# Self-attention of a decoder layer: the far corner of the weights moved to key quarters by transfers, outputs over 128 keys there, and a new written order

## The chip, the core and the metric

The kernel runs on one core of one Trainium2 chip. The metric is the device time of one execution in microseconds, lower is better. A core has five engines with queues of their own: TensorE (PE; its weight loads are shown as PEld), VectorE (DVE), ScalarE (ACT), GpSimd (POOL) and SyncE (SP), which here only issues transfers (DMAs). Everything is in float32.

## The reference

One decoder layer with normalization after each part: causal self-attention with rotary positions, cross-attention to a short context, and a feed-forward layer that only half of the tokens take. Two sequences of 1024 tokens, 256 channels, 16 heads of 64. The change touches the self-attention alone:

```python
q = split_heads(x @ Wq)
k = split_heads(x @ Wk)
v = split_heads(x @ Wv)
q = apply_rope(q)
k = apply_rope(k)
sim = jnp.einsum('bid,bjd->bij', q, k) * scale
causal = jnp.tril(jnp.ones((t, t), dtype=bool))
sim = jnp.where(causal[None], sim, -jnp.inf)
attn = jax.nn.softmax(sim, axis=-1)
out = jnp.einsum('bij,bjd->bid', attn, v)
out = out.reshape(b, h, t, d).transpose(0, 2, 1, 3).reshape(b, t, h * d)
return out @ Wo + bo
```

## The kernel before

Self-attention works on 16 pairs of heads (8 for each sequence), numbered n = 0 to 15; class `Pair` has a method for each step, and a step is written with a letter and digits. The 1024 tokens are eight tiles of 128. The steps of one pair:

- `Pk0`, `Pk1`, `Pq0`, `Pq1` (`project`, L268): keys and queries, half of the tokens each. `E..` (L276) takes them from PSUM on ScalarE; `d0`, `d1` (`swap`) send them through two transfers each so that neighbouring rows change places (`turned`); `c`, `s`, `a` (L288, L291, L295) apply the rotary tables on GpSimd.
- `Pv0`, `Pv4` (`values`, L303) and `Ev0`, `Ev4` (`kept`): values, a token tile of 128 keys on 128 partitions. `w` (`spread`) writes them to DRAM, and `l` (`copies`, L322) loads them back as `v4`, once for each of the four groups of 32 partitions: in row group r lie 32 keys of each quarter of a tile.
- `S0` to `S4` (`scores`, L342): scores of five groups of query tiles, (3, 1, 0), (4, 2), (5), (6), (7), both heads, 64 partitions each, into two PSUM tiles of which there are only two. `Tgj` (`least`, L355, VectorE) masks group g of head j, takes the row minima and frees the PSUM tile; `Xgj` (`exponentials`, L363, ScalarE) makes weights of them; `Rgj` (`turn`, L372, VectorE) writes them transposed in blocks of 32 x 32 into `p_t`. A block transpose leaves the query's quarter in the partition group and the key's quarter in the free index, so that of 128 keys only 32 stand on one group of partitions.
- `V0` to `V7` (`output`, L410): step n multiplies the weights of key tile n with its values. For key quarter k, head j and row group r there is one matmul of 32 keys by 64 columns, 32 in a step (20 in V7), and eight of them can run at once (four row groups, two column halves). Row group r adds into its own PSUM tile `po[r]`; the four take the whole ring of PSUM buffers from V0 to `O0` to `O3` (`gathered`, L424).
- `Q`, `I`, `D`, `B`, `M`, `W`: sums of the weights transposed, inverted, written to DRAM, loaded over the head's rows (`over`), multiplied in on GpSimd, and the pair's output stored.

Each of these matmuls is two instructions for TensorE, with a weight load each. The order of the work on all engines is written by hand. The list `steps` is one period, with the offset of the pair that each step works on: while the scores of pair n are made, V0 to V7 work on pair n-1 and the projections on pairs n+1 and n+2. The strings `opening` and `ending` spell out the first pairs and the last two, together with the output projection of the second sequence (`Closing`; letters A, C, Y, Z for the first sequence, f, F, g, z for the second, and U, which moves a projection from PSUM). The output projection of the first sequence, and its normalization, runs within the periods from pair 8 on. `2=` in the ending is two unread matmuls (`fill`).

`split` cuts some matmuls of scores and projections into two or four pieces, at most `pieces[n]` extra ones in pair n. `begin` issues a transfer on SyncE and, after V1 and V7, makes the next one wait for the outputs' last instruction (`gate`). SyncE, ScalarE's queue of transfers and the tables stand in program order: a waiting transfer holds up those behind it on its engine.

In the pools before, `p_t` is `[P, (NT + 1) * NT, P]`: 72 blocks, head 0 in an upper triangle (key tile, query tile), head 1 in the lower one. The constants `causal`, `ones`, `earlier` and the tiles `b2`, `w_r` live through the whole kernel; `ones`, `earlier`, `b2` and `w_r` are used only by the router and the feed-forward layer, after cross-attention has begun.

Of the kernel before, what the change touches and what calls it, by code (L numbers as in the profile page):

```python
# [34 lines left out]
def decoder_layer(  # L35
# [42 lines left out]

    ident = const.tile([P, P], F32)
    make_identity(nc, ident)  # L80
    causal = const.tile([P, P], F32)
    make_causal_mask(nc, causal, MASKED)
    neg_half = const.tile([P, 1], F32)
    G.memset(neg_half, -0.5)
    ones = const.tile([P, P], F32)
    G.memset(ones, 1.0)
    earlier = const.tile([P, P], F32)
    make_upper_triangular(nc, earlier, diag=False)
    place = const.tile([P, NT], F32)
    G.iota(place, [[P, NT]], 0, 1, allow_small_or_imprecise_dtypes=True)  # L90

# [36 lines left out]
        return po  # L128

    bo = const.tile([P, C], F32)  # L130
    b2 = const.tile([P, C], F32)
    b_r = const.tile([P, 1], F32)
    b1 = const.tile([P, NF], F32)
    w_r = const.tile([P, C], F32)
    cx = const.tile([S, B, C], F32)


# [1 line left out]

    keys = [(b, hp) for b in range(B) for hp in range(NP)]  # L140
    groups = [(3, 1, 0), (4, 2), (5,), (6,), (7,)]
    K4 = T // R32
    early = ctx.enter_context(ExitStack())
    e1 = early.enter_context(tc.tile_pool(name="early1", bufs=1, side="right"))
    e2 = early.enter_context(tc.tile_pool(name="early2", bufs=2, side="right"))
    with (
# [8 lines left out]

        fence = s1.tile([P, T], F32, name="fence")
        G.memset(fence[:, : T - P], 0.0)
        G.tensor_copy(fence[:, T - P :], causal)
        wo = s1.tile([P, NP, C], F32, name="wo")

        p_t = s1.tile([P, (NT + 1) * NT, P], F32, name="pT")
        attn_d = [dram.tile([NP, P, T], F32, tag="attn", name="attn_d") for _ in range(B)]
        x_ts = {}
        xs = [xpool.tile([P, NT, C + 1], F32, tag="x", name="x_0")]
# [1 line left out]
        def load(t, src):  # L166
            return lambda: nc.sync.dma_start(t, src)


        def load_next(h):  # L170
            if h == 0:
# [7 lines left out]
            0: [lambda: load_next(0)],  # L179
            1: [lambda: load_next(1)],  # L180
            2: [load(bo, L0_attn_bo.partition_broadcast(P))],
            3: [load(b2, L0_ffn_b2.partition_broadcast(P)), load(b_r, L0_ffn_b_r.partition_broadcast(P))],
            4: [
                load(w_r, L0_ffn_w_r.rearrange("c o -> (o c)").partition_broadcast(P)),
                load(b1, L0_ffn_b1.rearrange("(f p) -> p f", p=P)), load(cx, ctx_1024.rearrange("b s c -> s b c")),
            ],
            5: [load(wo[:, : NP // 2, :], outward[:, : NP // 2, :])],
# [29 lines left out]
        def begin(dst, src):  # L217

            ins = nc.sync.dma_start(dst, src)
            if gate:  # L220
                tc.add_manual_dep(ins.ins, gate.pop().ins.name, after, reason="the outputs' instructions come first")
# [3 lines left out]

        pieces = [2, 1, 13, 13, 11, 10, 11, 12, 13, 12, 8, 9, 8, 8, 9, 0]
        left = [pieces[0]]

        def split(first, last, most):
# [14 lines left out]
        class Pair:  # L246
# [60 lines left out]

            def kept(self, n):
                if self.v is None:
                    self.v = e1.tile([P, NT, P], F32, tag="v", name="v")  # L310
                    self.v_d = dram.tile([4, R32, NT * P], F32, tag="v", name="v_d")
                A.copy(self.v[:, n : n + NT // 2, :], self.pp["v", n])

            def spread(self):

                begin(self.v_d.rearrange("r k e -> (r k) e"), self.v.rearrange("p n d -> p (n d)"))

            def copies(self):

# [48 lines left out]
            def turn(self, g, j):  # L368
                for t, span in self.spans[g]:
                    first = (t, NT * (t + 1))[j]  # L370
                    step = (NT, 1)[j]
                    V.transpose(  # L372
                        p_t[:, first : first + t * step + 1 : step, :],
                        self.p[g, j][:, span].rearrange("p (n k) -> p n k", k=P),
                    )


            def sums_row(self):
# [20 lines left out]
            def output(self, n):  # L399
                if n == 0:  # L400
                    self.po = [ring.tile([P, NT, R32], F32, tag="t", name="po_self") for _ in range(4)]
                for k in range(4):
                    for j in range(2):
                        first = (NT * n + n, NT * (n + 1) + n)[j]
                        step = (1, NT)[j]
                        last = first + (NT - 1 - n) * step + 1

                        for r in range(k if n == NT - 1 else 0, 4):
                            rows = slice(r * R32, (r + 1) * R32)
                            ins = TE.matmul(  # L410
                                self.po[r][j * D : (j + 1) * D, n:, :],
                                self.v4[rows, NT * k + n, j * D : (j + 1) * D],
                                p_t[rows, first:last:step, k * R32 : (k + 1) * R32],
                                start=(n == 0 and k == 0), stop=(n == NT - 1 and k == r),
                            )
                if n in (1, NT - 1) and self.n < len(keys) - 1:
                    gate[:] = [ins]
                elif n == NT - 1:
                    final[:] = [ins]
# [20 lines left out]
        class Closing:  # L440
# [48 lines left out]


        steps = [
            ("Eq0", 1), ("Ek0", 1), ("Ev4", 1), ("Eq1", 1), ("a0", 0), ("R40", -1), ("S0", 0), ("T00", 0), ("T01", 0),
            ("s1", 0), ("V0", -1), ("a1", 0), ("V1", -1), ("d0", 1), ("B", -2), ("S1", 0), ("V2", -1), ("T10", 0),
            ("V3", -1), ("V4", -1), ("T11", 0), ("S2", 0), ("X00", 0), ("V5", -1), ("R00", 0), ("X01", 0), ("R01", 0),
            ("c0", 1), ("Z", -15), ("X11", 0), ("T20", 0), ("V6", -1), ("T21", 0), ("V7", -1), ("w", 1), ("X10", 0),
            ("X20", 0), ("O1", -1), ("S3", 0), ("R10", 0), ("O0", -1), ("R11", 0), ("Q", -1), ("s0", 1), ("O3", -1),
            ("T31", 0), ("l", 0), ("C", 0), ("O2", -1), ("X31", 0), ("Pk1", 1), ("T30", 0), ("I", -1), ("Pv0", 2),
            ("X30", 0), ("M", -2), ("R20", 0), ("Ek1", 1), ("d1", 1), ("R31", 0), ("Ev0", 2), ("D", -1), ("S4", 0),
            ("R30", 0), ("Pq1", 2), ("L", 3), ("W", -2), ("A", 0), ("c1", 1), ("X21", 0), ("Pq0", 2), ("T41", 0),
            ("Pk0", 2), ("X41", 0), ("T40", 0), ("R21", 0), ("R41", 0), ("X40", 0), ("Pv4", 2),  # L500
        ]

        pairs = [Pair(n) for n in range(len(keys))]
# [8 lines left out]
            "l": lambda a, x: a.copies(),  # L512
            "L": lambda a, x: a.weights(),
            "S": lambda a, x: a.scores(int(x)),
            "T": lambda a, x: a.least(int(x[0]), int(x[1])),
            "X": lambda a, x: a.exponentials(int(x[0]), int(x[1])),
            "R": lambda a, x: a.turn(int(x[0]), int(x[1])),
# [9 lines left out]


        opening = """
            1L 0Pk0 0Ek0 0Pq0 0Eq0 0H 0h 0Pq1 0c0 0d0 0s0 0a0 0Pk1 0Pv4 0Pv0 0Eq1 0S0 0Ek1 0Ev0 1Pk1 0T00 0d1 0Ev4 0T01  # L530
            1Pq1 0X00 0c1 0s1 0X01 1Eq1 1Ek1 1Pv0 0a1 0S1 2L 0R00 0w 0R01 1d1 1Pv4 1c1 1Pq0 1Pk0 0T10 0T11 0S2 1Ev4 0T21
            1Eq0 1Ek0 1d0 0X10 1Ev0 0l 1s1 1w 0X11 2Pq1 0T20 0R10 0S3 0R11 0X21 0X20 0T30 2Pk0 1a1 0T31 0X30 1c0 0S4
            0X31 0R20 1s0 0R30 0R21 1a0 2Eq1 0T40 3L 2Pv4 0T41 2Pv0 0X40 0X41 2Ek0 0R31 0R40 2Pq0 2Ev4 1S0 0R41 1T00
            2Eq0 2Ev0 0V0 1T01 0V1 2d0 0V2 1S1 1T11 0V3 1X00 0V4 0V5 1T10 1S2 1X01 1X11 1R00 0V6 0V7 2w 1X10 0O0 1T20
            1T21 1S3 1R10 1R01 0O1 2c0 1l 1X20 1T31 2Pk1 0O3 1T30 0O2 3Pv4 0Q 2Ek1 1S4 2c1 1X30 2s0 1X21 3Pq1 1R20 3Ev4
            3Pv0 2a0 1R11 3Pk0 0I 1T41 2d1 1R30 1X31 3Pq0 1T40 2S0 1R21 1X41 1X40 1R31 1R40 0D 1R41 2T00 3Ek0 2s1 3Eq1
            4L 2a1 3Eq0 3Ev0 1V0 1V1 3d0 0B 2T01 2X00 1V2 2S1 1V3 1V4 2T10 2T11 1V5 2R00 2S2 2X01 2T20 2T21 1V6 2X11
            2R01 1V7 3c0
        """


        ending = """
            14X10 12M 14X20 14S3 13O0 15s0 14X21 14R11 14R20 14l 13O1 14T31 14T30 14R21 14X30 14X31 15Pk1 15w 13Q 13I
            14S4 15Ek1 14T40 12W 4C 14T41 14X41 13O2 14R10 15a0 15d1 14R31 13O3 14R30 13D 14X40 15c1 14R40 14R41 15S0 4Y
            15T00 14V0 15T01 15X00 14V1 14V2 15X01 15s1 15a1 14V3 5A 13B 15R00 15S1 15T10 14V4 6A 15X10 14V5 15T11 15S2
            14V6 14V7 15X11 15R01 15T21 15l 15T20 13M 14O3 15S3 7A 15X20 5C 15X21 15R10 15T30 14O0 15T31 15R11 15X30
            15R21 14O1 15R30 15X31 13W 15S4 15R20 15T41 15T40 14Q 5U 14O2 15X41 14I 15R31 15X40 6C 15Q 2= 14D 15I 15R40
            6U 15R41 15V0 4Z 14B 5Y 15V1 15V2 0f 15V3 14M 1f 7C 15V4 15V5 5Z 6Y 15V6 6Z 15D 15V7 15B 2f 15O1 15O3 7U 0n
            15O2 15O0 0F 1F 2F 3f 1g 3F 2g 3g 7Y 4f 3z 0N 5f 7Z 4F 5F 1z 6f 6F 4g 0g 7f 2z 5g 5z 4z 6g 7F 7g 1N 6z 7z 0z
        """  # L550
        closings = [[Closing(b, i) for i in range(NT)] for b in range(B)]
        closing = {
# [118 lines left out]
    wqk = c1.tile([P, NC, B, H, S], F32, name="wqk")  # L671
    packed = [c1.tile([P, NK, C], F32, name=f"packed_{b}") for b in range(B)]
    vo_d = dram.tile([B, HS, C], F32, tag="vo", name="vo_d", bufs=1)

    class Prepare:
        def __init__(self):
# [479 lines left out]
```

## Time and profile before

| | us |
|---|---|
| median of 3 runs (808.66 to 815.99) | 810.68 |
| profiled execution, its own time | 809.84 |
| span of the profiled execution | 808.1 |
| granted TensorE clock, mean | 0.998 |

Busy time of the engines in stretches of the profiled span (us; the last three columns are the granted clock, the share of time that the 16 DMA engines were busy, and the bytes moved):

| stretch | what | PE | DVE | ACT | POOL | clock | DMA | GB/s |
|---|---|---|---|---|---|---|---|---|
| 0 to 60 | opening | 57.46 | 30.66 | 29.10 | 26.79 | 1.00 | 0.52 | 159 |
| 60 to 120 | opening, pairs 1 and 2 | 58.01 | 45.98 | 33.76 | 30.63 | 1.00 | 0.59 | 173 |
| 246.7 to 276.5 | one period, first sequence | 29.50 | 22.74 | 17.05 | 16.43 | 1.00 | 0.65 | 194 |
| 406 to 439 | one period, with an output projection | 33.00 | 24.08 | 17.14 | 17.63 | 1.00 | 0.61 | 177 |
| 439 to 500 | last full periods and ending | 56.20 | 48.74 | 29.43 | 33.54 | 1.00 | 0.59 | 159 |
| 500 to 527 | last pair | 25.06 | 16.64 | 7.28 | 6.01 | 1.00 | 0.67 | 171 |
| 527 to 555 | output projection, second sequence | 28.00 | 13.00 | 0.24 | 7.96 | 1.00 | 0.67 | 235 |
| 555 to 808 | cross-attention, router, feed-forward | | | | | | | |

In the profile, `x<-y` names what an instruction writes and reads, `32*64` the rows and columns of the array that a matmul uses, and a wait is put down to the event that ended it. The chain of waits is the work that ended last, followed back from the end. "issue" in it is time in which TensorE waited for nothing that the profile shows. The groups of the changed line before, kept apart by shape (count, busy us, mean ns of one, then idle time before it and what ended that):

```
L410 PE MATMUL po_self<-pT,v 32*64 32x256 f32 x1024 | 33.6, 381 | 2.2 <-DMA inv_d<-inv 1.1 <-DVE pT L372 0.7 <-DMA v<-v_d 0.4
L410 PE MATMUL po_self<-pT,v 32*64 32x224 f32 x1024 | 28.2, 347 | 0.0
L410 PE MATMUL po_self<-pT,v 32*64 32x128 f32 x1024 | 21.2, 275 | 2.6 <-issue 2.4
L410 PE MATMUL po_self<-pT,v 32*64 32x64 f32 x1024 | 18.4, 231 | 3.4 <-issue 2.9
L410 PE MATMUL po_self<-pT,v 32*64 32x32 f32 x640 | 13.1, 219 | 0.3 <-issue 0.3
```

### The profile page before, as it was taken

The page shows a single profiled execution, that of the slowest core. Times are in us where ns is not written, and L with a number is a line of the kernel's source. Part 1 is how long each engine was busy: PE and PEld are TensorE (multiplying, and loading weights), DVE is VectorE, ACT ScalarE, POOL GpSimd, SP SyncE. Part 2 cuts the span into 40 slices and gives each one's busy share as a digit, 9 for nine tenths or more (in the row PEclk, how much of TensorE's full clock was granted, in tenths as well). Part 3 has the DMA queues.
Part 4 walks back from the last instruction along what each step waited for, and adds up shares of the span by engine and source line. Part 5 has one row for each costly group of instructions (what it writes and reads, how often), then busy time and mean ns, then how long its engine had stood idle before and what let it go on. Part 6 is the DMA issues. An engine that isn't in the chain of part 4 may idle for free.

```text
span 808.1 us, 26591 instructions
## 1 busy us (share of the span) xinstructions
PE 781.5 (97%) x11428; PEld 622.0 (77%) x11428; DVE 581.9 (72%) x1345; ACT 355.4 (44%) x842; POOL 367.7 (45%) x261
## 2 busy tenths in 40 slices
PE   8999999999999999999999988999999999999986
PEld 5565888888888888788788776688788888886745
DVE  2578678868778868678667796535577788888674
ACT  2565565655565556454554544102433332333130
POOL 2634455555375565365473553222033222261664
PEclk9999999999999999999999999999999999999999
DMA  5455477557567567668366467690450000011221
GB/s 195 129 148 177 129 210 209 171 168 211 157 169 230 158 179 223 174 171 204 112 198 185 133 185 158 173 324 3 168 187 1 1 1 0 1 53 53 68 91 52
DMA packets 65328, 112.32 MB, mean 139 GB/s; under 512 B 6497, under 2 KB 43707, under 8 KB 65211
## 3 DMA queue, kind: packets, MB, share of 16 engines
q1 hardware_dynamic: 59067, 89.64, 37.6%
q10 hardware_dynamic: 4608, 16.78, 7.5%
q0 software_dynamic: 1536, 4.20, 1.4%
q8 instruction: 90, 1.47, 0.8%
q14 instruction: 27, 0.22, 0.1%
HBM read 71.24 MB, written 22.59 MB: 116 GB/s over the span
## 4 chain that ended last, share of the span: by engine, by line
PE 82%; DVE 7%; POOL 4%; issue 4%; ACT 1%; DMA 1%; POOLq 0%; SPq 0%; ACTq 0%; DVEq 0%
PE po_self L410 17%; PE ps_scores L342 16%; PE pp_kq L268 13%; PE pp_v L303 7%; PE po_cross L998 6%; PE ps_cross L946 6%; PE po_proj L477 6%; PE pp_h L889 3%; PE po_ffn L900 2%; PE pt_p L978 1%; DVE pT L372 1%; DMA turned<-raw 1%; POOL comp L831 1%; POOL e L967 1%; DVE p L355 1%
## 5 line engine op out<-in xcount | busy, mean ns | idle before, releaser
L363 ACT ACTIVATE p<-p,neg 128x768 f32<-128x768 f32 (+7 forms) x256 | 196.3, 768 | 162.9 <-DVE neg L355 161.3
L355 DVE CUSTOM_DVE_ANT_0 p<-ps_scores,fence 128x512 f32<-128x512 f32 (+7 forms) x256 | 179.4, 750 | 104.9 <-PE ps_scores L342 104.5
L372 DVE STREAM_TRANSPOSE pT<-p 128x512 f32<-128x512 f32 (+7 forms) x256 | 175.7, 740 | 6.2 <-PE po_self L410 3.0
L410 PE MATMUL po_self<-pT,v 32*64 32x256 f32 (+6 forms) x7808 | 157.6, 295 | 10.1 <-issue 7.2
L410 PEld LDWEIGHTS po_self<-pT,v 32*64 32x64 f32 x7808 | 137.2, 130 | 34.9 <-issue 25.4
L342 PE MATMUL ps_scores<-kq 64*128 64x256 f32 (+3 forms) x1060 | 148.9, 411 | 1.8 <-DVE neg L355 1.0
L342 PEld LDWEIGHTS ps_scores<-kq 64*128 64x128 f32 x1060 | 93.3, 186 | 42.7 <-issue 28.2
L268 PE MATMUL pp_kq<-xT,w_pair 128*128 128x256 f32 (+2 forms) x524 | 118.6, 379 | 1.1 <-ACT xT L203 0.7
L291 POOL TENSOR_TENSOR turned<-turned,sin 128x1024 f32<-128x1024 f32 x31 | 73.2, 2362 | 93.0 <-DMA turned<-raw 80.1
L288 POOL TENSOR_TENSOR kq<-raw,cos 128x1024 f32<-128x1024 f32 x31 | 73.6, 2374 | 84.4 <-ACT raw L276 84.4
L268 PEld LDWEIGHTS pp_kq<-xT,w_pair 128*128 128x128 f32 x524 | 88.3, 190 | 23.9 <-issue 10.4
L967 POOL TENSOR_TENSOR e<-e,inv 128x616 f32<-128x616 f32 x32 | 38.2, 1215 | 113.0 <-DVE inv L966 67.2
L120 POOL TENSOR_TENSOR rs<-ve,neg_half 128x1 f32<-128x1 f32 x48 | 27.2, 570 | 107.2 <-DVE ve L118 105.2
L295 POOL TENSOR_TENSOR kq<-kq,turned 128x1024 f32<-128x1024 f32 x31 | 73.5, 2371 | 1.4
L998 PE MATMUL po_cross<-packed,pT 128*128 128x256 f32 (+1 forms) x320 | 72.5, 380 | 0.1
L946 PE MATMUL ps_cross<-wqk,x1T 128*128 128x308 f32 x256 | 69.2, 423 | 0.0
L998 PEld LDWEIGHTS po_cross<-packed,pT 128*128 128x128 f32 (+1 forms) x320 | 60.0, 190 | 9.4 <-ACT pT L984 0.3
L303 PEld LDWEIGHTS pp_v<-w_pair,xT 128*128 128x128 f32 x512 | 61.1, 192 | 4.0 <-issue 2.5
L303 PE MATMUL pp_v<-w_pair,xT 128*128 128x128 f32 x512 | 62.2, 275 | 0.0
L946 PEld LDWEIGHTS ps_cross<-wqk,x1T 128*128 128x128 f32 x256 | 47.4, 190 | 16.2 <-issue 0.7
L959 ACT ACTIVATE e<-e 128x616 f32<-128x616 f32 x32 | 23.0, 717 | 80.8 <-DVE e L955 80.8
L477 PE MATMUL po_proj<-wo,attnT 128*128 128x256 f32 x224 | 51.4, 381 | 0.3 <-ACT out_pair L424 0.3
(128 smaller groups left out, 817.0 us busy)
## 6 DMA issues: line engine op xcount, KB each, us to landing
turned<-raw SPq DMA_DIRECT2D x64, 256.0 KB, 4.7
v<-v_d ACTq DMA_DIRECT2D x32, 512.0 KB, 6.2
v<-v_d SPq DMA_DIRECT2D x32, 512.0 KB, 11.1
v_d<-v SPq DMA_DIRECT2D x16, 512.0 KB, 4.6
over<-inv_d SPq DMA_DIRECT2D x32, 256.0 KB, 4.8
attn_d<-out_pair SPq DMA_DIRECT2D x14, 512.0 KB, 4.3
attnT<-attn_d SPq DMA_DIRECT2D x8, 512.0 KB, 5.4
vo_d<-vo SPq DMA_DIRECT2D x2, 1232.0 KB
```

Of the source, the lines that this page charges most:

```text
L268: TE.matmul(pp[:, cols], self.w[:, c, "kq".index(of), :], x_ts[self.b, n][:, c, cols], start=(c == 0), stop=(c == NC - 1),)
L288: E.tensor_tensor(self.kq[:, :, n * NB : (n + 1) * NB], self.raw[n], self.twice(cos, n), ALU.mult)
L295: E.tensor_tensor(dst, dst, self.turned[n], ALU.add)
L303: TE.matmul(pv[:, i, :], x_ts[self.b, 2 * n // NT][:, c, toks], self.w[:, c, 2, :], start=(c == 0), stop=(c == NC - 1),)
L342: TE.matmul(self.ps[j][:, cols], self.kq[rows, 1, t * P : (t + 1) * P], self.kq[rows, 0, cols.start - at : cols.stop - at], start=True, st ...
L355: V.tensor_tensor_reduce(p[:, span], self.ps[j][:, span], fence[:, T - (t + 1) * P :], -SCALE, -MASKED, ALU.add, ALU.min, neg[:, i : i + 1],)
L363: A.activation(p[:, span], p[:, span], AF.Exp, bias=neg[:, i : i + 1], scale=-1.0, accum_out=self.sums[:, j, t : t + 1],)
L372: V.transpose(p_t[:, first : first + t * step + 1 : step, :], self.p[g, j][:, span].rearrange("p (n k) -> p n k", k=P),)
L410: ins = TE.matmul(self.po[r][j * D : (j + 1) * D, n:, :], self.v4[rows, NT * k + n, j * D : (j + 1) * D], p_t[rows, first:last:step, k * R ...
L477: TE.matmul(self.po, of, wo[:, c, :], start=(c == 0), stop=(c == NP - 1))
L946: TE.matmul(ps[:, g, : Q * S], self.x_t[:, c, :], wqk[:, c, self.b, h : h + Q, :].rearrange("p h s -> p (h s)"), start=(c == 0), stop=(c = ...
L998: TE.matmul(po, self.p_t[:w, k, :], packed[self.b][:w, k, :], start=(k == 0), stop=(k == NK - 1))
```

## The change

`p_t` is laid out with the key quarter first, `[P, 4, 72, 32]`. A new step `J` (`joined`) sends the far corner of the weights, key tiles 4 to 7 by query tiles 4 to 7 of both heads, through sixteen transfers on SyncE into a new tile `far`: from row group r, key quarter k to partition group k, query quarter r. There the 128 keys of a tile stand on 128 partitions. V4 to V7 then take 8 matmuls each (query quarter, head) of 128 keys by 64 columns, with the values as `kept` left them; V0 to V3 stay as they were. Only the first four tiles of values are spread and copied (`K4` is halved), and the values are two tiles, `v[0]` and `v[4]`. The matmuls of scores and projections are no longer split after the first pair. `steps`, `opening` and `ending` are written anew, with V4 after S2. `2=` is gone. `ones`, `earlier`, `b2` and `w_r` move behind self-attention; the causal mask is written into `fence` at once.

```diff
-    K4 = T // R32
+    K4 = T // R32 // 2
...
-        p_t = s1.tile([P, (NT + 1) * NT, P], F32, name="pT")
+        p_t = s1.tile([P, 4, (NT + 1) * NT, R32], F32, name="pT")
+        far = s1.tile([P, 4, NT // 2 + 1, NT // 2, R32], F32, name="far")
...
-        pieces = [2, 1, 13, 13, 11, 10, 11, 12, 13, 12, 8, 9, 8, 8, 9, 0]
+        pieces = [2, 0, 0, 0, 0, 0, 0, 0, 0, 0, 0, 0, 0, 0, 0, 0]
...
                     V.transpose(
-                        p_t[:, first : first + t * step + 1 : step, :],
-                        self.p[g, j][:, span].rearrange("p (n k) -> p n k", k=P),
+                        p_t[:, :, first : first + t * step + 1 : step, :].rearrange("p c n q -> p n c q"),
+                        self.p[g, j][:, span].rearrange("p (n c q) -> p n c q", c=4, q=R32),
                     )
+
+            def joined(self):
+
+                for k in range(4):
+                    for r in range(4):
+                        begin(
+                            far[k * R32 : (k + 1) * R32, r, :, :, :].rearrange("p m t q -> p m (t q)"),
+                            p_t[r * R32 : (r + 1) * R32, k, NH * NT :, :].rearrange("p (m t) q -> p m (t q)", t=NT)[:, :, NH * R32 :],
+                        )
...
+                heads = [slice(j * D, (j + 1) * D) for j in range(2)]
+                if n < NH:
+                    for k in range(4):
+                        for j, cols in enumerate(heads):
+                            for r in range(4):
+                                rows = slice(r * R32, (r + 1) * R32)
+                                ins = TE.matmul(
+                                    self.po[r][cols, n:, :], self.v4[rows, NH * k + n, cols],
+                                    p_t[rows, k, across(j, n, NT), :], start=(n == 0 and k == 0), stop=False,
+                                )
+                else:
+                    for r in range(4):
+                        for j, cols in enumerate(heads):
                             ins = TE.matmul(
+                                self.po[r][cols, n:, :], self.v[NH][:, n - NH, cols],
+                                far[:, r, :, :, :].rearrange("p m t q -> p (m t) q")[:, across(j, n - NH, NH), :],
+                                start=False, stop=(n == NT - 1),
                             )
...
-            ("Eq0", 1), ("Ek0", 1), ("Ev4", 1), ("Eq1", 1), ("a0", 0), ("R40", -1), ("S0", 0), ("T00", 0), ("T01", 0),
-            ("s1", 0), ("V0", -1), ("a1", 0), ("V1", -1), ("d0", 1), ("B", -2), ("S1", 0), ("V2", -1), ("T10", 0),
-            ("V3", -1), ("V4", -1), ("T11", 0), ("S2", 0), ("X00", 0), ("V5", -1), ("R00", 0), ("X01", 0), ("R01", 0),
...
-            ("R30", 0), ("Pq1", 2), ("L", 3), ("W", -2), ("A", 0), ("c1", 1), ("X21", 0), ("Pq0", 2), ("T41", 0),
-            ("Pk0", 2), ("X41", 0), ("T40", 0), ("R21", 0), ("R41", 0), ("X40", 0), ("Pv4", 2),
+            ("Ev4", 1), ("R40", -1), ("a0", 0), ("Eq0", 1), ("J", -1), ("Eq1", 1), ("Ek0", 1), ("S0", 0), ("T01", 0),
+            ("X01", 0), ("d0", 1), ("V0", -1), ("B", -2), ("V1", -1), ("T00", 0), ("s1", 0), ("a1", 0), ("S1", 0),
+            ("V2", -1), ("V3", -1), ("T11", 0), ("c0", 1), ("T10", 0), ("S2", 0), ("V4", -1), ("Z", -15), ("R01", 0),
+            ("T20", 0), ("X00", 0), ("V5", -1), ("R00", 0), ("V6", -1), ("X11", 0), ("X10", 0), ("T21", 0), ("V7", -1),
...
+            ("I", -1), ("Ev0", 2), ("S4", 0), ("D", -1), ("M", -2), ("W", -2), ("R30", 0), ("s0", 1), ("T41", 0),
+            ("Ek1", 1), ("Pv4", 2), ("Pq1", 2), ("R31", 0), ("d1", 1), ("A", 0), ("X41", 0), ("Pq0", 2), ("T40", 0),
+            ("c1", 1), ("L", 3), ("X21", 0), ("R20", 0), ("X40", 0), ("R21", 0), ("R41", 0), ("Pk0", 2),
...
-            14V6 14V7 15X11 15R01 15T21 15l 15T20 13M 14O3 15S3 7A 15X20 5C 15X21 15R10 15T30 14O0 15T31 15R11 15X30
-            15R21 14O1 15R30 15X31 13W 15S4 15R20 15T41 15T40 14Q 5U 14O2 15X41 14I 15R31 15X40 6C 15Q 2= 14D 15I 15R40
-            6U 15R41 15V0 4Z 14B 5Y 15V1 15V2 0f 15V3 14M 1f 7C 15V4 15V5 5Z 6Y 15V6 6Z 15D 15V7 15B 2f 15O1 15O3 7U 0n
+            15X20 13W 15S4 15R30 15R10 14Q 15R20 15X31 15T41 15T40 14O1 14O2 15X41 14I 15R31 15X40 15R40 6C 6U 5U 7A 14D
+            15Q 15R41 15V0 0f 15V1 1f 15I 14B 4Z 14M 15V2 7C 15V3 5Y 6Y 15D 15J 15V4 5Z 15V5 15V6 15B 15V7 2f 15O2 15O0
...
+    ones = c1.tile([P, P], F32, name="ones")
+    G.memset(ones, 1.0)
+    earlier = c1.tile([P, P], F32, name="earlier")
+    make_upper_triangular(nc, earlier, diag=False)
+    b2 = c1.tile([P, C], F32, name="b2")
+    w_r = c1.tile([P, C], F32, name="w_r")
+    nc.sync.dma_start(w_r, L0_ffn_w_r.rearrange("c o -> (o c)").partition_broadcast(P))
+    nc.sync.dma_start(b2, L0_ffn_b2.partition_broadcast(P))
```

## The prediction

> **What bounds the kernel now.** I read the busy shares and the chain of waits of the page first, then the chain of one period of self-attention, then the timeline of VectorE and SyncE, then the transfers' landing times.
>
> ```profile
> PE 781.5 (97%) x11428; PEld 622.0 (77%) x11428; DVE 581.9 (72%) x1345; ACT 355.4 (44%) x842; POOL 367.7 (45%) x261
> ...
> PE 82%; DVE 7%; POOL 4%; issue 4%; ACT 1%; DMA 1%; POOLq 0%; SPq 0%; ACTq 0%; DVEq 0%
> ```
>
> TensorE is busy 97% of the span and carries 82% of the chain. The change touches self-attention, the first 526 us. There one head pair is one period; this is most of the chain of one (start, length, what):
>
> ```profile
> 250.28 1.93 PE ps_scores L342 x16
> 252.21 5.38 PE pp_kq L268 x24
> 257.58 1.78 PE pp_v L303 x16
> 259.37 1.73 PE ps_scores L342 x20
> 261.10 3.43 PE po_self L410 x128
> 264.53 1.93 PE ps_scores L342 x12
> 266.45 2.96 PE po_self L410 x146
> 269.42 0.17 issue
> 269.59 0.96 PE po_self L410 x43
> 270.55 1.49 PE ps_scores L342 x8
> 272.04 1.08 PE po_self L410 x58
> 273.12 0.13 issue
> 273.25 1.36 PE po_self L410 x78
> ```
>
> No other engine stands in it: the period is TensorE's own work, one `issue` gap apart. The outputs (L410) are V0 and V1 (261.10, 3.43 us), V2 to V4 (266.45 to 270.55, 4.10 us), V5 to V7 (272.04 to 274.62, 2.58 us). The period, from 244.78 to 274.62, is 29.84 us; the seven from 111.55 to 320.46 (starts of V0) average the same. VectorE is busy 22.8 us of such a period.
>
> ```profile
> 225.62 3.23 DVE L372 STREAM_TRANSPOSE pT<-p 128x768 f32<-128x768 f32 x3
> ...
> 241.82 0.96 DVE L355 CUSTOM_DVE_ANT_0 p<-ps_scores,fence 128x768 f32<-128x768 f32 x1
> ...
> 224.72 0.40 SPq L219 DMA_DIRECT2D w_pair<-in_L_attn_Wk_dram  x1
> 225.18 0.46 SPq L219 DMA_DIRECT2D w_pair<-in_L_attn_Wq_dram  x1
> ```
>
> ```profile
> turned<-raw SPq DMA_DIRECT2D x2, 256.0 KB, 2.3
> turned<-raw SPq DMA_DIRECT2D x64, 256.0 KB, 4.7
> ```
>
> A transfer costs SyncE about 0.4 to 0.6 us to issue. From SBUF to SBUF it lands after 2.3 us with nothing else in flight (the two of 50 to 62 us), after 4.7 us in the median of all.
>
> **Part by part. The outputs over 128 keys.** V0 to V3 keep their 32 matmuls each (832 of the 1152 columns that a round streams). V4 to V7 go from 32, 32, 32 and 20 matmuls of 32 keys, eight at a time, to 8 each of 128 keys, two at a time: the array's work stays, the count falls from 116 to 32. The price before: V0 and V1 stream 480 columns in 3.43 us, 7.1 ns a column; V2 and V3 (352) so take 2.45 us, and V4 to V7 took 4.10 - 2.45 + 2.58 = 4.2 us for 320 columns. At the pace of V0 and V1 they need 320 x 7.1 ns = 2.3 us; the last two, of 64 and 32 columns, cannot shrink with their columns, since each matmul still loads its weights, so I take 2.7 us. Bounds: 2.3 us, and 4.5 us if two half-width tiles do not overlap (320 columns x 16 instructions each, at the 1.15 columns a ns of L303's sixteen instructions of 128 in 1.78 us). Gain: 1.5 us a period, between 1.9 and -0.3.
>
> No row shows 128 x 64 tiles. The nearest are the 32 x 64 ones of V0, two column halves in each row group at full pace, and the full 128 x 128 ones of L303, whose 61.1 us of weight loads lie within 62.2 us of matmuls. So loads do overlap matmuls on the same rows.
>
> The Trainium skill, "TensorE: Matmul & The Clock Gate", Part 3, says under "What overlaps and what doesn't" that a weight load overlaps matmuls in flight only when its row group differs. All loads of V4 to V7 would then stand alone, and the sum would be the slow bound above or more; the row of L303 speaks against it.
>
> **The splits.** Pieces of 256 columns took 5.38 us for three projections, 1.79 each; the unsplit ones of the opening take 1.72 to 1.91 each. Nothing (+-0.1 us a period). The `issue` gaps, 0.3 us here and in V4 to V7, are in the 4.2 us already.
>
> **The written order.** It makes a new wait. Let 0 be the start of a period's first scores, with the lengths above. S0 to 1.73, V0 and V1 to 5.16, S1 to 7.09, V2 and V3 to 9.54. S2 needs T11 and T10 (2.5 us on VectorE, 236.78 to 239.30, behind S1): it starts at 9.7 and ends at 11.2. Now V4 to V7 follow at once, to 13.9, but S3 needs T20 and T21: VectorE does R01 (1.23, by the 2.34 us of six in 239.43), T20 (0.95) from 11.3, R00 (1.23), T21 (0.95), to 14.5. So S3 waits 0.6 us. Then S3 1.72, the sums' row 0.21, projections and values 1.79 and 1.78, S4 1.93 (it ends at 21.9), values 1.78, three projections 5.38: the period is 29.1 us, 0.7 less than before. Of the 1.5 us the two VectorE waits take back 0.8.
>
> **The transfers (J).** Sixteen a pair, on SyncE, after R40. From S4's end VectorE does T41, R31, T40, R20, R21, R41, R40: 1.2 + 1.1 + 1.2 + 0.9 + 0.9 + 1.2 + 1.2 = 7.7 us (the 3.23 us of three above are 0.9, 1.2, 1.2), so R40 ends at 0.5 of the next period and J starts at 0.6. V4 comes at 11.2; its last quarter may land 0.6 us later, and S3's wait hides another 0.6: J may take 11.8 us unpunished. No transfer of 32 partitions in 512-byte runs with this end is in the trace; the nearest are the weights' loads (same runs; 0.46 us and 0.05 to the next) and the 0.52 to 0.6 us of `turned`. I take 0.56 us: 15 x 0.56 + 2.3 = 10.7 us, hidden under V0 to S2. The program gives all transfers eight semaphores in turn, so the ninth waits for the first to land; at 2.3 us that costs nothing. Bounds: 15 x 0.45 + 2.3 = 9.1 us, and with 4.7 us of landing 15 x 0.58 + 4.7 = 13.4 us, 1.6 over.
>
> Behind J in SyncE's queue stand the swap of the next pair (needed by s0, half a period later), the loads of `over` (needed by the scaling after V7) and the spread of v: each has over 8 us of cover; without it J's 9 us of issuing would fall on them. VectorE's R11 waits for J too, at 14.5: later than J by the same sum. Bytes: J adds 16 x 80 = 1280 KB; the spread and copies of v lose 256 and 1024 KB. No more traffic; the copies, 11.1 us to landing, lie elsewhere in the period.
>
> **VectorE's and TensorE's other patterns** (128-byte runs written by the transposes): same elements, taken as no cost; bounds -0.2 and +0.5 us a period. **Moved constants:** two loads, a memset and a mask go behind self-attention, where GpSimd waits 28.1 us (L967 for ACT) and SyncE 27.7 us (L95): nothing; uncovered some 4 us once.
>
> **Opening.** J there has V0 to V3 and S1, 7.8 us, before V4, plus 0.7 us between R41 and V0. Two pairs each wait 10.7 - 0.6 - 8.5 = 1.6 us and gain 1.5 or more: 0, between -2 and +6.
>
> **Ending.** J of the last pair is queued behind the loads of `over` for pair 14, which wait for its inverse sums to land (3.6 us; 508.07), and behind its own: it starts about 3.3 us after the last transposes and ends at 14.0. Before V4 stand V0 to V3 and a projection: 5.9 + 3.7 = 9.6. So 14.0 - 0.6 - 9.6 = 3.8 us of wait, less 1.5 gained: +2, between 0 and +6.
>
> **Sum.** 12 periods x -0.7 = -8.4 (those from 330 us on have 3.5 us of output projection more, before and after), opening 0, ending +2: -6.4. The profiled span of 808.1 becomes 801.7; the execution was 809.84, 1.7 more: 803.4. It lay 0.8 under the median of 810.68. Forecast 803.
>
> **Rivals.**
> *J comes late (slower).* If transfers land after 4.7 us, as the median one does, J takes 13.4 us and each period loses 1.6: 29.1 + 1.6 = 30.7, 12 x 0.86 = +10, opening 2 x (4.3 - 1.5) = +6, ending +4: 808.1 + 20 + 1.7 = 830. It decides from 11.8 us of J on; the break-even is 12.5 us. For it: the loads of the next weights are issued just before J, and `turned` took 8.9 us in a busy stretch (119 to 140 us). Against: the copies that made that stretch busy lie elsewhere, and the quiet pair landed in 2.3. A mild form, J of 12.3 us: -0.2 a period, opening and ending +6: 813.
> *Half-width tiles do not overlap.* V4 to V7 take 4.5, S3 starts at 15.7, the period is 30.3: 12 x 0.46 + 6 = +11: 821. V0's pace speaks against it.
> *VectorE does not hold S2 and S3 back.* TensorE's own sum is 28.3 us a period: -18 + 1, so 793. VectorE is busy only 22.8 of 29.8 us, but its chain from S1 to T21 has no slack in the rows.
>
> **How the numbers follow.** Forecast, J hidden (797 to 808): 0.47. VectorE no hindrance: 0.11. Mild J, 807 to 819: 0.13. J late: 0.21. No overlap: 0.08. One per cent, about what a measurement of this kernel can tell from no change, is 802.6 to 818.8. Faster: 0.26 of the forecast's and 0.11: 0.37. Slower: 0.20 + 0.07 = 0.27, and 0.04 of the mild case: 0.31. Same: 0.32. The range, 791 to 834, leaves out a tenth at each end.
>
> **What would show it.** Right: V4 to V7 in one block of 2.7 us; periods of 29.1 us; no wait of L422 for a transfer in mid-kernel, a short one before S3 for the minima, one of 3 to 4 us in the last pair. Wrong: L422 waiting for `far` in every period (J late), SyncE issues of `far` over 0.6 us or with waits in them, V4 at over 1.5 us (no overlap), or periods near 28.3 us.

## The result and the profile after

| | before | after |
|---|---|---|
| median (4 runs each, side by side) | 813.34 (808.66 to 817.08) | 844.17 (843.12 to 845.3) |
| ratio, 95% interval | | 1.0382 (1.0317 to 1.0448) |
| span of the profiled execution, its own time | 808.1, 809.84 | 841.3, 843.12 |
| granted TensorE clock, mean | 0.998 | 0.982 |

The change made the kernel 3.8% slower; the forecast was 803 us, with a range up to 834. The page of the changed kernel, busy shares and chain of waits:

```profile
PE 786.5 (93%) x8184; PEld 553.2 (66%) x8184; DVE 580.5 (69%) x1345; ACT 354.1 (42%) x842; POOL 366.3 (44%) x260
...
PE 48%; SPq 21%; DVE 19%; DMA 5%; issue 4%; POOL 2%; ACT 1%; POOLq 0%; ACTq 0%; DVEq 0%
```

TensorE carries 48% of the chain in place of 82%, and SyncE's queue, which was at 0%, 21%. What TensorE waited for (total us, times, the longest):

```profile
PE po_self L422 <- DMA far<-pT: 31.0, 45, 3.5
PE ps_scores L335 <- POOL kq L287: 4.0, 1, 4.0
PE po_proj L488 <- DVE out_pair L441: 2.1, 1, 2.1
```

L422 is V4 to V7, `far` the tile that J fills; the other two waits stand once each, in the ending. One period of TensorE and the same stretch of SyncE's queue (start, length, count; in brackets the idle time before and what ended it):

```profile
309.68 1.78 PE L335 MATMUL ps_scores<-kq 64*128 64x512 f32 x12
...
319.35 1.66 PE L335 MATMUL ps_scores<-kq 64*128 64x512 f32 x8
322.54 1.19 PE L422 MATMUL po_self<-far,v 128*64 128x128 f32 x12 [1.53 <-DMA far<-pT]
324.04 2.00 PE L422 MATMUL po_self<-far,v 128*64 128x128 f32 x52 [0.31 <-DMA far<-pT]
325.97 1.77 PE L335 MATMUL ps_scores<-kq 64*128 64x512 f32 x8
```

```profile
310.08 12.29 SPq L211 DMA_DIRECT2D far<-pT  x16
```

J starts 0.4 us into the period and SyncE issues for 12.29 us. S2 ends at 321.0. V4 then waits 1.53 us until its first quarter of the queries has landed, and 0.31 more for its last. The chain of the same period shows J one transfer at a time:

```profile
312.78 0.60 SPq L211
313.38 0.04 issue
313.43 1.59 SPq L211
315.01 0.04 issue
315.06 0.60 SPq L211
...
321.12 0.60 SPq L211
321.72 0.04 issue
321.77 2.14 DMA far<-pT
```

Most take 0.60 us, the first two 0.67 and 0.65, two of the sixteen 1.59 and 1.50; 0.04 stand between two. The last lands 2.14 us after its start. J is 323.9 - 310.1 = 13.8 us. From V0 of pair 2 on, the shortest periods of the first sequence became 30.6 to 30.9 us, the others 32 to 34; in two of these the clock comes in. Two stretches of the changed kernel; the third number from the end is PEclk, the granted clock:

```profile
193.40:196.80 3.40, 1.38 (x14) 0.78 (x15) 2.62 (x8) 0.00 (x0) 0.00 (x0) 0.99 0.51 149
196.80:200.20 3.40, 3.40 (x52) 3.40 (x52) 1.23 (x2) 0.44 (x2) 0.00 (x0) 0.50 0.84 263
```

After 3.4 us in which TensorE was busy for 1.38, the next 3.4 run at half clock: a half-clock window. There are eight such windows before 565 us, where before had none. Clock time lost over the span (half of the time at half clock) is 16.1 us against 2.7.

Where the 33.2 us of span arose, by TensorE's blocks: up to V0 of pair 2 +9.0 (111.55 to 120.56 us); the eleven periods to V0 of pair 13 +16.4 (341.52 to 357.97); from there to the end of the last V7 +4.5; everything behind +3.3, mostly the wait of 2.1 us above and a half-clock window (1.7) in the output projection.

The ending's waits are J's too, by way of SyncE's queue. J of pair 13 holds it from 477.2 to 489.2; the loads of `over` for pair 12 are issued behind it, from 490.6, and land after 7.3 us (4.3 in the median). GpSimd waits 15.9 us for them, to 498.6, and the rotation that it does next is late for S0 of pair 15, which waits 4.0 us. The 2.1 us before the output projection end the same way, with `over` issued behind the last J. In e1 (below), where J is a quarter, the loads for pair 12 are issued 8.8 us earlier, counted from V0 of pair 13, and neither wait is there.

### The profile page after: what moved, and what is told of

It reads as the page before. It is cut to its first block, busy times and chain, and to the rows that moved or that the text cites. A ratio compares the mean times of both kernels' runs of the same rounds, so it can differ in the third digit from the quotient of the medians.

```text
span 841.3 us, 20385 instructions
## 1 busy us (share of the span) xinstructions
PE 786.5 (93%) x8184; PEld 553.2 (66%) x8184; DVE 580.5 (69%) x1345; ACT 354.1 (42%) x842; POOL 366.3 (44%) x260
## 4 chain that ended last, share of the span: by engine, by line
PE 48%; SPq 21%; DVE 19%; DMA 5%; issue 4%; POOL 2%; ACT 1%; POOLq 0%; ACTq 0%; DVEq 0%
SPq L211 21%; DVE pT L365 9%; PE ps_scores L335 8%; PE po_cross L1019 6%; PE ps_cross L967 6%; PE po_proj L488 5%; DVE p L348 5%; PE pp_kq L260 4%; PE po_self L422 4%; DMA far<-pT 4%; PE pp_v L295 4%; PE pp_h L910 3%; PE po_ffn L921 2%; PE pt_p L999 1%; POOL e L988 1%
## 5 line engine op out<-in xcount | busy, mean ns | idle before, releaser
L356 ACT ACTIVATE p<-p,neg 128x1024 f32<-128x1024 f32 (+7 forms) x256 | 196.2, 768 | 149.2 <-DVE neg L348 146.5
L365 DVE STREAM_TRANSPOSE pT<-p 128x640 f32<-128x640 f32 (+7 forms) x256 | 179.9, 748 | 14.1 <-PE po_self L415 6.3
L335 PE MATMUL ps_scores<-kq 64*128 64x512 f32 (+3 forms) x768 | 153.2, 515 | 4.0 <-POOL kq L287 4.0
L260 PE MATMUL pp_kq<-xT,w_pair 128*128 128x512 f32 (+1 forms) x264 | 116.4, 582 | 1.1 <-ACT xT L195 0.8
L415 PE MATMUL po_self<-pT,v 32*64 32x224 f32 (+3 forms) x4096 | 102.0, 344 | 2.5 <-DVE pT L365 1.3
L444 POOL TENSOR_TENSOR out_pair<-out_pair,over 128x1024 f32<-128x1024 f32 x15 | 35.5, 2368 | 157.3 <-DMA over<-inv_d 157.3
L415 PEld LDWEIGHTS po_self<-pT,v 32*64 32x64 f32 x4096 | 85.2, 133 | 18.7 <-issue 8.8
L422 PE MATMUL po_self<-far,v 128*64 128x32 f32 (+3 forms) x1024 | 57.1, 258 | 31.9 <-DMA far<-pT 31.0
L260 PEld LDWEIGHTS pp_kq<-xT,w_pair 128*128 128x128 f32 x264 | 47.8, 190 | 47.5 <-issue 40.5
L422 PEld LDWEIGHTS po_self<-far,v 128*64 128x64 f32 x1024 | 44.8, 147 | 49.2 <-issue 29.2
```

The lines of the kernel that those rows point to most:

```text
L260: TE.matmul(pp[:, cols], self.w[:, c, "kq".index(of), :], x_ts[self.b, n][:, c, cols], start=(c == 0), stop=(c == NC - 1),)
L335: TE.matmul(self.ps[j][:, cols], self.kq[rows, 1, t * P : (t + 1) * P], self.kq[rows, 0, cols.start - at : cols.stop - at], start=True, st ...
L356: A.activation(p[:, span], p[:, span], AF.Exp, bias=neg[:, i : i + 1], scale=-1.0, accum_out=self.sums[:, j, t : t + 1],)
L365: V.transpose(p_t[:, :, first : first + t * step + 1 : step, :].rearrange("p c n q -> p n c q"), self.p[g, j][:, span].rearrange("p (n c q ...
L415: ins = TE.matmul(self.po[r][cols, n:, :], self.v4[rows, NH * k + n, cols], p_t[rows, k, across(j, n, NT), :], start=(n == 0 and k == 0), ...
L422: ins = TE.matmul(self.po[r][cols, n:, :], self.v[NH][:, n - NH, cols], far[:, r, :, :, :].rearrange("p m t q -> p (m t) q")[:, across(j, ...
```

## The experiments

**A quarter of J** (e1), **two queues** (e2), **the order alone** (e3), **no pieces** (e4). One set, against 809.75 us of before; the edits are shortened.

```diff
 e1            def joined(self):
-                for k in range(4):
+                for k in range(1):          # far set to 0.0 once
 e2                 for r in range(half, 4, 2):
-                        begin(
+                        (begin, nc.scalar.dma_start)[half](
 e3  K4, kept, copies and output of before; joined returns at once
 e4  -pieces = [2, 1, 13, 13, 11, 10, 11, 12, 13, 12, 8, 9, 8, 8, 9, 0]   (in before)
     +pieces = [2, 0, 0, 0, 0, 0, 0, 0, 0, 0, 0, 0, 0, 0, 0, 0]
```

> The changed kernel with J cut to 4 of its 16 transfers (those of the first quarter of the weights' partitions); the other three quarters of `far` hold zeros, so the far outputs leave out three quarters of their sum, while TensorE's instructions stay as they are. Theory 1 (J is too long on one queue: 16 issues of 0.65 us and two pauses make 13.8 us where 11.8 are free): J takes about 3 x 0.65 + 2.3 = 4.3 us, no wait of L422 for `far` in mid-kernel, periods of 29.1 to 29.4 us against 30.6 to 33 in the changed kernel, no clock windows at 0.5 in mid-kernel, 798 to 810 us in all. Theory 2 (the new written order itself costs, and J only stands where another wait would): periods stay at 30 us or more and the time at 830 or more. Theory 3 (the clock's drops come from something other than J's waits): windows at 0.5 remain at three or more places before 565 us, time 815 to 830.

795.01 us, ratio 0.9815 (0.977 to 0.986). No wait for `far`, undisturbed periods of 28.73 us, one half-clock window before 620 us. Taking J's time away is worth some 49 us (46 by the two ratios) and turns the change into a gain: theory 1, and 3 us under its range.

> The changed kernel with all 16 transfers of J, eight issued by SyncE and eight by ScalarE. Theory 1 (issuing on one queue is what is long): eight issues of 0.65 us and a landing of 2.3 to 3.5 us make 6.9 to 9 us, under the 11.8 that are free: no wait of L422 for `far` in mid-kernel, periods of 29.1 to 29.6 us, 798 to 812 us in all; the 5 us a period that ScalarE issues are covered, it is busy 42%. Theory 1b (the landing and its shared semaphores make the pauses, whoever issues): J stays at 11 to 14 us, periods of 30 us or more, over 825 us. Theory 2 (the order costs): 830 or more. A mishap would be ScalarE's exponentials coming late by 5 us: the transposes R then wait for ACT and the periods grow by up to 3 us.

801.43 us, 0.9899 (0.9846 to 0.9952). In mid-kernel TensorE never waits for `far`, and undisturbed periods are 28.73 to 28.75 us too. All sixteen transfers are made, with the same bytes: one queue's issuing was what was long. The mishap came true in one place, the ending:

```profile
466.94 7.71 ACTq L374 DMA_DIRECT2D far<-pT  x8
474.69 0.72 ACT L356 ACTIVATE p<-p,neg 128x512 f32<-128x512 f32 x1 [9.72 <-DMA far<-pT]
```

ScalarE issues for 7.7 us, its exponentials start only then, the transposes and minima of VectorE behind them too, and S2 of pair 15 waits 1.94 us for them.

> The kernel before, with no product of pairs 1 to 14 split in pieces. Theory 1: nothing, within 0.1 us a period: 809 to 813 us. Theory 3 (the splits kept TensorE's queue fed, and their removal is part of the loss): 1 us a period or more, 822 us or more.

836.27 us, 1.0345 (1.0288 to 1.0401): the pieces are worth 26 us in the kernel before: theory 3. TensorE's wait for `issue` there, and a stretch of its timeline:

```profile
PE po_self L410 <- issue: 25.1, 20, 2.6
```

```profile
276.13 3.40 PE L410 MATMUL po_self<-pT,v 32*64 32x192 f32 x177
281.99 0.47 PE L410 MATMUL po_self<-pT,v 32*64 32x128 f32 x15 [2.46 <-issue]
```

Before had 7.2 us of that wait, 13 times. From 120 to 420 us the gaps stand after matmuls number 1738, 1866, 2373, 2880, 3514, 3642, 4656, 5417, 6431 and 7192 of TensorE's stream: the distances are 1, 4, 5, 6 or 8 times 126.8. The pages name the cause, in their list of queues:

```profile
q8 instruction: 86, 1.41, 0.7%
```

Here it made 86 transfers of 16 KB, in before 90, in after 65. TensorE's instructions (two for a matmul, and its semaphore instructions) number 22,027, 23,140 and 16,653: 256.1, 257.1 and 256.2 a transfer. So a transfer brings 256 instructions, and 126.8 matmuls with their waits are one block. In all twelve traces no two of these transfers begin less than 3.25 us apart once 20 us have passed, while 232 matmuls of V4 to V7 pass in 3.1 where nothing stops them (e3, below), so a block of them in 1.7: it is used up before the next is there. In the gap at 279.53 a block's transfer begins at 279.51 and ends at 280.74, and TensorE goes on 1.25 us later. So do the others: each of the 55 gaps of over 0.3 us in before, e3, e4 and e5 ends 1.22 to 1.61 us after the end of such a transfer. A piece more or less moves the block's end; that the pieces put it behind the short matmuls is read from the gaps they save, not tried piece by piece.

> The new written order, layout of the weights, removed splits and moved constants, but the far outputs over 32 keys as before and no J: V4 to V7 are 116 matmuls of 32 keys again. Theory 1 (the order costs no more than the two VectorE waits worked out beforehand): V4 to V7 at 4.2 us cover S3's wait of 0.6, so the period is 29.1 + 1.5 - 0.6 = 30.0 us, 12 x 0.16 = 2 us over before, opening and ending 0 to 4 us: 810 to 818 us. Theory 2 (the order is what costs): 828 or more, periods of 30.6 us or more with waits of TensorE for VectorE or ScalarE.

838.11 us, 1.0346 (1.029 to 1.0403), as slow as the changed kernel without one transfer of J. That looks like theory 2, but L407, the outputs, waits 20.3 us for `issue` here, nearly always within V6 and V7, and there are nine half-clock windows. The profiled span is 29.9 us longer than before's; 13.1 more of `issue` and 15.4 more of lost clock time (18.1 against 2.7) come to about that. A period without a gap is 28.8 to 28.9 us (151.93 to 180.79, 245.80 to 274.62), in which V4 to V7 take 3.1; in e4, with the order of before and no pieces either, the shortest is 29.1. So in mid-kernel the order itself doesn't cost.

**The order with the pieces** (e5), **J with two fifths of its bytes** (e6, one execution), **matmuls in front of V4** (e7), **two queues, ending mended** (e8). Against 812.37 us of before.

```diff
 e5  (e3)  pieces of before
 e6        far[..., r, :2, :, :] <- p_t[..., k, NH * NT : (NH + 2) * NT, :]   # 32 KB, not 80
 e7                 else:
+                    for _ in range(4 if n == NH else 0):
+                        TE.matmul(self.po[0][:, NH:, :], ident, fence[:, : NH * R32], start=False, stop=False)
 e8  (e2)  r outside, k inside; r 0 and 2 on SyncE, 1 and 3 on ScalarE
-            14J 5A ... 14V3 15X01 15S1
+            14J 14j0 5A ... 14V3 15X01 14j1 15S1     # pair 14: ten on SyncE, 3 + 3 on ScalarE
```

> The run of the order alone (32-key outputs, no J), with the pieces of the kernel before put back. That run lost 28 us and the kernel before without its pieces lost 26, both in `issue` gaps of 1.2 to 2.6 us inside V5 to V7, 126.8 matmuls or a multiple of it apart. Theory A (the pieces move those gaps out of the 32-key outputs, and the order itself costs nothing): 808 to 820 us, the sum of L407's issue gaps back from 20.3 us to under 10. Theory B (the order itself costs): 828 us or more, with the gaps gone all the same.

829.28 us, 1.0192 (1.015 to 1.0233): by the time in theory B's place, but without its sign, since 13.8 us of `issue` gaps remain (these pieces were laid out for another order). There are waits of 1 to 2 us for ScalarE and of up to 0.3 for GpSimd's rotation. How much of the 17 us is the order's own and how much gaps stays open; a set of pieces made for it wasn't tried.

> The changed kernel with all 16 transfers of J on SyncE, but each with the first two of its five runs a partition (32 KB in place of 80 KB); the rest of `far` holds zeros, so three fifths of the far weights are left out of the outputs. Theory A (the issue costs what its number of runs costs, and the pauses come from runs still in flight): spacing 0.3 to 0.45 us, no pauses, J at most 9 us, no waits for `far`, 793 to 802 us. Theory B (the issue costs a fixed 0.6 us a transfer): J stays at 12 to 14 us, 835 us or more.

833.08 us. The issues are 0.596 us in the median (0.602 with all bytes), and the longer ones, of some 1.3 us, are there as well, two or three of nearly every sixteen. SyncE's queue for a pair:

```profile
234.34 12.40 SPq L212 DMA_DIRECT2D far<-pT  x16
```

Theory B: the time of issuing goes by the number of transfers, not by runs or bytes. Fewer bytes help a little at the other end: a transfer lands after 1.9 us in place of 2.1, and the wait for `far` is 25.8 us in place of 31.0.

> The changed kernel, with four matmuls of 256 columns against zeros (they add nothing to the outputs) in front of V4, some 1.5 us in which TensorE would wait for J anyway. Theory A (the windows at half clock come from TensorE's idle time before V4): the windows in mid-kernel and in the opening (63.6, 97.8, 196.8, 261.6) vanish, 844 falls by 4 to 12 us. Theory B (they come from something else): the windows stay and the time is 842 to 852.

839.64 us, 1.0302 (1.0256 to 1.0348), which overlaps the changed kernel's interval; six windows were left in the profiled execution (846.42 us, the longest of the four). The wait for `far` is 17.6 us in place of 31.0, but up to 2.0 at a time. Inconclusive: the fill was too short for the opening's waits. The traces settle it better. Over before, after and the ten kernels of this study there are 43 half-clock windows from 20 to 620 us, and in the 3.4 us ahead of each TensorE was idle for at least 1.37; gaps in code loading bring them as well as waits for J. From the kernel without pieces (e4):

```profile
376.40:379.80 3.40, 1.17 (x29) 0.53 (x16) 2.15 (x7) 1.94 (x6) 1.14 (x2) 1.00 0.00 0
379.80:383.20 3.40, 3.40 (x89) 2.24 (x87) 1.47 (x3) 0.41 (x1) 0.00 (x0) 0.50 0.03 7
```

Not every gap of over 2 us is followed by one (2.6 us at 545.3 in that kernel is not). The traces show on what it depends: in each of them all windows begin whole multiples of 3.413 us apart. Cut by this grid, from 20 to 620 us, every full-clock step with 1.80 us of idle time or more is followed by a half-clock one (32 steps), none with less than 1.37 is, and of those between 11 are and 19 are not. The gap at 545.3 lies across two steps, with 1.74 us of idle time in the first.

> The run with two queues, with the transfers in the order of V4's reading (the quarter of queries outermost) and, for pair 14 in the ending, ten on SyncE and six on ScalarE, three of them before and three after the exponentials X00 and X01 of pair 15. There the eight issues in one piece kept ScalarE for 7 us, S2 of pair 15 waited 1.9 us for the minima, the clock fell to 0.5 for 6.8 us twice and pair 15's V0 came 5.6 us later than with a quarter of the transfers. Theory A (that piece is the cause): 795 to 799 us, 1.3 to 2% under the kernel before. Theory B (the ending waits for the transfers themselves): 800 to 803 us.

796.16 us, 0.9791 (0.9761 to 0.9822; one of six executions, of 1585.66 us, stands outside the comparison): 2.1% under before (1.8 to 2.4), with all of `far` moved. Theory A. Mid-kernel is as in e2 (332.03 against 332.18 us from V0 of pair 2 to that of pair 13), so the new order of the transfers brings nothing there; V0 of pair 15 follows that of pair 14 after 28.24 us in place of 33.83. A period of it:

```profile
263.31 1.66 PE L335 MATMUL ps_scores<-kq 64*128 64x512 f32 x8
264.90 2.66 PE L425 MATMUL po_self<-far,v 128*64 128x128 f32 x64
267.49 2.20 PE L335 MATMUL ps_scores<-kq 64*128 64x512 f32 x8
```

```profile
254.04 7.31 SPq L211 DMA_DIRECT2D far<-pT  x8
```

V4 to V7 follow S2 at once, in one block to 267.49; S3 takes 2.13 us in place of 1.72, held up by the minima. On either queue eight issues take 5.4 to 7.9 us, where half of the 12.3 for sixteen on one queue would be 6.2.

**The old order** (e9), **the pieces put back** (e10), both in e8, against 807.22 us of before.

```diff
 e9   steps, opening, ending of before, with J and j right behind the last R of a pair
 e10  pieces of before
```

> The version on two queues with the written order of before (opening, steps and ending), J placed right behind the last transposes; far outputs over 128 keys, no pieces. Theory A (the gain is the 128-key outputs', and the order only has to leave room for J): the transfers take some 9.2 us, V4 comes 9.7 us after R40 in that order, so 795 to 806 us. Theory B (the new order is itself part of the gain, or is what makes room for J): waits of L425's line for `far` in every period, 812 us or more.

823.95 us, 1.0207 (1.0147 to 1.0266): by the time in theory B's place, but without its sign, since L425 waits for `far` 1.3 us in all. In mid-kernel theory A holds: V0 of pairs 2 to 13 lie 333.68 us apart (e8: 332.03, before: 341.52). The loss is in the opening and the ending:

```profile
PE po_proj L491 <- DVE out_pair L444: 7.3, 1, 7.3
PE po_self L418 <- ACT raw L268: 5.0, 1, 5.0
PE po_self L418 <- DMA far<-pT: 4.8, 1, 4.8
```

The 5.0 us are my placement: the eight issues stand before two evacuations of ScalarE there. So 128 keys and two queues bring the periods' gain in either order; in the opening and the ending, as placed here, J costs more than that.

> The version on two queues with the pieces of the kernel before put back. Theory A (with V4 to V7 in 32 matmuls of 128 keys, no run of matmuls is short enough to outrun what `issue` stands for, so the pieces have nothing left to save): 796 to 801 us, at most 0.3 us a period more, from products of 256 columns at 1.79 us in place of 1.72. Theory B (the pieces still save gaps): under 793 us.

799.22 us, 0.9889 (0.9838 to 0.994), 3 us over e8's median of another set, as the profiled spans are (796.0 and 793.0); against each set's own before it is 1% more. Periods are 28.88 us in place of 28.73, and in neither do the outputs have an `issue` gap of over 0.3 us. Theory A: nothing to save.

## Why the prediction was wrong

- *J of 10.7 us* is the step that failed. From one issue to the next it is 0.647 us in the median, not 0.56: 15 x 0.647 = 9.7. Two issues of a pair, sometimes three, take 1.0 to 1.9 us, some 2 us more in all; the landing, 2.14 against 2.3, was right. 13.8 in all. The 0.56 were taken from transfers of other shapes; "over 0.6 us or with waits in them" stood among the signs of being wrong, but not in the bounds: the upper one, 13.4, was built on a slow landing. The eight semaphores cost nothing, as forecast: eight issues take over 5 us, and a transfer lands after 2.1 to 4.1.
- *J may take 11.8 us unpunished*: right. 13.8 - 11.8 = 2.0, and the period without waits, 28.73, grew to 30.7.
- *Rival "J comes late"*: right in what happens and in the period's price (30.7), wrong in the cause, issuing and not landing, and too low in the sum: 830. The clock, 16.1 - 2.7 = 13.4 us, stood in no case of mine; with it the rival comes to 843, though its opening (+6) and ending (+4) were themselves short or wide of +9.0 and +4.5, so the match proves little.
- *V4 to V7 at 2.7 us*: right, 2.59. *The rival that half-width tiles do not overlap* is out: at the slow bound they would take 4.5. So is the Trainium skill's rule ("TensorE: Matmul & The Clock Gate", Part 3, "What overlaps and what doesn't") as I read it; here 64 loads of 137 ns and their matmuls on all 128 rows pass in 2.66 us (e8), so loads overlap matmuls of the same rows, and the measurement decides.
- *V4 to V7 cost 4.2 us before*: that period held two stalls, of some 0.5 and 0.4 us, of which the lines show 0.17 and 0.13 as `issue`. V2 to V4 took 4.10 us there and V5 to V7 2.58; in a period of before without stalls (V0 at 141.15) they take 3.56 and 2.19. V2 and V3 alone take 2.60 (e3), not 2.45 (at the rate of V0 and V1 it would be 2.52). So V4 to V7 take some 3.1 us of work, and 128 keys save 0.5 of it (2.59); the stalls are a gain of their own, and the changed kernel has no `issue` gap of over 0.3 us in its outputs.
- *The splits: nothing*: true only beside the 128-key outputs (e10: putting them back saves nothing). The sum took the `issue` gaps for a constant of the outputs; without the splits the old outputs lose 26 us (e4).
- *VectorE takes back 0.8 us a period*: half. S2 does not wait, S3 loses 0.4 in its second half (e8). The third rival, no hindrance, gave 793, and e1 and e8, without J's wait, are at 795 and 796.
- *Opening 0, ending +2*: J's size again, 3.3 and 3.5 us of wait for the two pairs of the opening, and half-clock windows behind them at 63.6 and 97.8 us. In the ending the place was wrong: V4 of the last pair, forecast to wait 3.8 us, waits 0.4.
- *Each has over 8 us of cover* (the transfers behind J in SyncE's queue): it held in mid-kernel. In the ending the loads of `over` had none, and S0 of pair 15 and the output projection waited 4.0 and 2.1 us behind them, a term the sum put at nothing.

## What to carry to other kernels

Price a batch of transfers by count times the issue time of the queue in such a batch, pauses included, and compare it with the room before its first reader; where it is over, a second queue shortens it (12.3 us to some 7 here), if the engine that owns the queue has nothing due in that time. Look also at what is queued behind the batch. Where a stretch of short matmuls shows `issue` gaps at equal distances in TensorE's instruction stream, count instructions before touching anything that shifts them. Put a price on the clock too: a wait of some 2 us can cost 1.7 more, half of the window that may follow.

## What was not expected of the hardware

- From one issue of J to the next it is 0.64 to 0.65 us whether a transfer has 64 or 160 runs of 512 bytes. One in five to fourteen transfers, mostly five to nine, takes 1.0 to 1.9 us, and it and the two before it land after 2.6 to 4.0 us in place of 2.1. What the pause is, no run here shows.
- TensorE's code comes in blocks of 256 instructions, 16 KB, no two beginning within 3.25 us; a block takes 0.9 to 1.9 us to move, and where TensorE had run out, it went on 1.2 to 1.6 us after that. 127 matmuls of 32 keys can pass in 1.7 us.
- Half-clock windows begin on a grid of 3.413 us and followed steps of it with 1.37 to 3.4 us of idle time, always from 1.80 on. The Trainium skill ("TensorE: Matmul & The Clock Gate", "HAM oscillation — how this bites in real kernels") gives the rule of no idle gaps over about 3.4 us; here shorter ones were enough, depending on how they lay in the grid.
